# Golay bits of four tiles in one product, one row mean, paired chances, a reordered setup and later leads

## The chip, the cores and the metric

The kernel runs on one core of a Trainium2 chip. The metric is the device time of one execution, in microseconds (us), median of several runs. Engines: PE multiplies matrices, DVE and ACT work element by element, POOL issues the gathers and scatters by index, SP issues the plain DMAs. Every engine works through its own instructions in order and waits on semaphores of the others.

## The reference

x is 16 x 1024 x 512, that is 16384 tokens. D is one scalar, made from the first 1024 elements.

```python
xn = _layernorm(x, axis=-1)
x1 = jnp.fft.ifft(jnp.fft.fft(xn, axis=-1) * filt(D), axis=-1).real
bits = (sigmoid(x1 @ W_el + b_el) > 0.5)                  # 24 a token
syn = (bits @ _H.T > 0.5)                                 # 12 a token
corrected = where(0 < syn.sum(-1) <= 3, bits flipped at the set places, bits)
s = x1 + corrected @ W_le + b_le
probs = softmax(xn @ router_w.T)                          # 8 experts, two chosen
w = topk_vals / (topk_vals.sum(-1, keepdims=True) + 1e-06)
g = silu(sum over the two of (xn @ expert_w[e] + probs[e]) * w[e])
out = x + s * g
```

## The kernel before

The 16384 tokens are 128 tiles of 128 tokens; a block is TPT = 4 tiles, a group GT = 8 tiles, a routing round 16 tiles.

**Setup** finds D, and from it the filter's matrices cs, cd and cm, whose first columns also give the 24 code logits and the 8 router logits. `constants` and `more_constants` fill small tables; `setup` issues the rest in an order written by hand, with the first tiles' `total`, `spread`, `fold` and `transpose` among it.

**Pass 1** (`pass_1`, L1050 on) takes the tiles in turn. Per tile: `total` adds the halves of x and the row's sum on DVE (L431); `spread` squares on ACT for the variance (L451); `level` makes two scalings of four tiles' sums, k.low = -4/E times the sum (L444) and the mean, column 10 of the record (L445); `scale` gives the reciprocal deviation; `fold` makes sums and differences, sd on DVE (L490, L493) and mm on POOL (L495); `transpose` turns these four blocks on PE (L502) and ACT copies them to pmt (L504); `filt` multiplies on PE (L518, L519, L521) and ACT scales the result into yb (L524); each block is stored to yd, which also starts a load of a later block and, for the first eight, of one expert's weights. How far totals and spreads run ahead is set by AHEAD_S = 11 and by a ramp at the start (2g+13 and 2g+12).

The Golay code, `code(s)`, is worked once a group: bits (L560), `turn_bits` for four tiles at a time (one matmul of 24 columns a tile, L569, and one ACT copy, L572), `syndrome` (one matmul a tile, L579), `correct` (L583 to L593). Its steps go out one a tile. `route(n)` goes out up to four steps a tile: the two largest logits, the softmax's chances and weights, 28 pair indicators (L709, one product for each distance between experts), sums over four tiles (L723), each token's rank in its pair's list by PE (L731 to L755), place (L762), row numbers (L767), and then 16 scatters to `lists` (L771). `put_records` stores the records.

**Pass 2** (the loop on L1383) first works `whole` tiles, 128 tokens of one pair of experts: two products of four f32 matmuls, PE L1228, scaled on ACT (L1275), added on DVE (L1278), silu on ACT (L1279). Leftover tokens go by expert: 61 `item` tiles with one product each, stored to ed; later `rest` tiles gather these parts. The order is 28 whole, 61 items, 5 whole, then 27 rest among 68 whole. Each step issues for later tiles: entries of the lists (AHEAD_K = 9 tiles ahead), x rows (6), parts (4), yd rows (5), `normalize` (L1189, 4), `turn` (four transposes and ACT's xt copy, L1196 and L1198, 2 ahead). `turn_code` turns the corrected bits (L1249, copy ct L1253), `mend` multiplies by W_le, `spread_out` joins the parts of x1 on DVE, `combine` and `put` finish and scatter the rows. `routes` and `aside` hold list work that goes out one or more steps a tile at the start of pass 2.

The changed kernel has functions of the same names; the diff below says what is in them.

Of the kernel before, what the change touches and what calls it, by code (L numbers as in the profile page):

```python
# [17 lines left out]
P = 128  # L18
PSUM = bass.MemoryType.PSUM
DRAM = bass.MemoryType.DRAM  # L20
NPAIR = 28
# [6 lines left out]
def pairs_of(ne=8):  # L28

    return [(a, a + d) for d in range(1, ne) for a in range(ne - d)]  # L30
# [3 lines left out]
def kernel(  # L34
# [114 lines left out]
    ht_b = p1c.tile([L, 12], BF16, name="ht_b")  # L149
# [15 lines left out]
    ht = sp.tile([L, 12], F32, name="ht")  # L165
# [23 lines left out]
    def constants():  # L189
# [26 lines left out]
        kf = kf[:, 0:KC]  # L216
# [13 lines left out]
        v.memset(eps, EPS)  # L230

    def more_constants():
# [11 lines left out]
        for r in recs:  # L244
            g.memset(r, 0.0)
            g.memset(bits_of(r)[:, :, L : L + 1], 1.0)
        for py in pys:
            v.memset(py[:, 1, X + H : WY], 0.0)

    def setup():  # L250
# [19 lines left out]
        nc.tensor.matmul(pm[:, NS - 1 :], st.own, sums[:, NS - 1 :], start=True, stop=True)  # L270
        above = sp.tile([P, NS, HW], F32, name="above")
# [7 lines left out]
        nc.tensor.matmul(pn, st.all, cnt, start=True, stop=True)  # L279
        ly = sp.tile([P, NS], F32, name="ly")  # L280
        v.tensor_scalar(ly, pn, 1.0, None, ALU.max)
        nc.scalar.activation(ly, ly, AF.Ln)
# [19 lines left out]
        v.tensor_sub(wt[:, 2:4, :], lat[:, 0:2, :], lat[:, 2:4, :])  # L302
        gain = sp.tile([P, KC], F32, name="gain")
# [10 lines left out]
        for i in range(2):  # L314
            for c in range(2):
                nc.tensor.matmul(
                    pys[1][:, i, 0:H], bas[:, 2 + c, i * P : (i + 1) * P], gbas[:, 2 + c, :],
                    start=(c == 0), stop=(c == 1),
                )
        v.tensor_add(wt[:, 0, :], wp[:, 0, :], wp[:, 1, :])  # L320
        v.tensor_sub(wt[:, 1, :], wp[:, 0, :], wp[:, 1, :])
        for g in range(2):
            total(g)
            spread(g)
        nc.scalar.copy(cs[:, X:], pys[0][:, 0, 0:Q])
        nc.scalar.copy(cd[:, X:], pys[0][:, 1, 0:Q])
        for g in range(2, 4):
            total(g)
            spread(g)
        level()  # L330
        nc.scalar.copy(cm[:, :, X:], pys[1][:, :, 0:H])
# [3 lines left out]
        fold(0)  # L335
# [12 lines left out]
        for op in scale(0, slice(0, TPT)):  # L348
            op()
# [3 lines left out]
        for g in range(4, GT):  # L353
            total(g)
            spread(g)
        level()
# [65 lines left out]
    def total(g: int):  # L422

        k, j = groups[g // GT], g % GT
        if j == 0:
            k.sum = small.tile([P, GT], F32, name="sum")
            k.sq2 = small.tile([P, GT], F32, name="sq2")
            k.low = small.tile([P, GT], F32, name="low")
# [12 lines left out]
    def level():  # L441
        while means:
            k, js = means.pop()
            nc.scalar.activation(k.low[:, js], k.sum[:, js], AF.Copy, scale=-4.0 / E)  # L444
            nc.scalar.activation(k.rec[:, js, 10], k.sum[:, js], AF.Copy, scale=1.0 / E)  # L445
# [38 lines left out]
    def fold(g: int):  # L484
# [6 lines left out]
            sd[:, 0:Q], p[:, 0:Q], k.low[:, j : j + 1], p[:, Q:H], ALU.add, ALU.add  # L491
# [61 lines left out]
    def code(s: int):  # L553
# [3 lines left out]
        def bits():  # L557

            k.bits = bits_of(k.rec)[:, :, 0:L]
# [4 lines left out]
        def turn_bits(h):  # L564
            if h == 0:
                k.bt = small.tile([L, GT, P], BF16, name="bt", bufs=2)
            pg = ps_g.tile([P, 512], F32, name="pg")[0:L].rearrange("l (j t) -> l j t", t=P)
            for j in range(TPT):
                nc.tensor.matmul(  # L569
                    pg[:, j, :], k.bits[:, h + j, :], ident_b, start=True, stop=True  # L570
                )
            nc.scalar.copy(k.bt[:, h : h + TPT, :], pg)  # L572

        def syndrome():
            k.pg = ps_g.tile([P, 512], F32, name="pg")[:, 0 : GT * 12].rearrange(
                "p (j n) -> p j n", n=12
            )
            for j in range(GT):
                nc.tensor.matmul(k.pg[:, j, :], k.bt[:, j, :], ht_b, start=True, stop=True)  # L579

        def correct():
# [12 lines left out]
                k.bits[:, :, 0:12], k.bits[:, :, 0:12], fix, ALU.not_equal  # L594
# [20 lines left out]
    def route(n: int):  # L615
# [30 lines left out]
        def total():  # L646
            st.sm = new("sm", [P, S])
# [886 lines left out]
```

## Time and profile before

| | |
|---|---|
| four runs | 1461.28, 1461.63, 1444.55, 1458.19 us; median 1459.74 |
| profiled execution | 1460.7 us, of which 1458.8 are its span; mean granted clock 0.967 |
| PE, DVE, POOL, ACT busy | 1344.1, 924.3, 876.7, 604.1 us |
| read from HBM, written | 144.79 MB, 87.75 MB |

A window row gives a stretch and its length, then for each engine its busy time and the number of instructions, PE's granted clock (1.00 is full), the share of DMA and what it moved in GB/s. The whole span in six stretches: setup, the DMA-bound tiles, the other tiles of pass 1, the start of pass 2 with 28 whole tiles, the items, the rest.

```profile
0.00:40.00 40.00, 24.68 (x121) 20.78 (x122) 28.62 (x135) 29.04 (x78) 13.46 (x44) 0.91 0.63 217
40.00:120.86 80.86, 77.89 (x491) 62.31 (x490) 71.23 (x262) 73.85 (x179) 40.53 (x48) 0.98 1.01 342
120.86:312.00 191.14, 184.97 (x1179) 146.87 (x1178) 174.67 (x642) 172.20 (x410) 146.57 (x162) 0.98 0.70 219
312.00:606.00 294.00, 250.63 (x781) 124.22 (x780) 175.84 (x460) 77.23 (x139) 154.34 (x146) 0.93 0.33 98
606.00:866.00 260.00, 242.07 (x740) 119.22 (x739) 41.94 (x84) 65.81 (x124) 117.82 (x117) 0.97 0.43 131
866.00:1458.80 592.80, 563.83 (x1641) 271.42 (x1639) 432.01 (x1058) 185.93 (x369) 403.99 (x365) 0.98 0.52 156
```

Engine columns: PE, PE's weight loads, DVE, ACT, POOL.

### The profile page before, as it was taken

How to read it: one execution, taken by the hardware profiler on the slowest of the kernel's cores; microseconds unless marked ns; L12 is line 12 of the kernel's file. 1: busy time of each engine (PE TensorE's matmuls, PEld its weight loads, DVE VectorE, ACT ScalarE, POOL GpSimd, SP SyncE). 2: the span in 40 equal slices, each digit the busy share in tenths (PEclk: the TensorE clock that was granted, in tenths of full speed). 3: DMA queues.
4: the chain of work that ended last, by engine and by line, in shares of the span. 5: the costliest groups of instructions: out<-in, count | busy, mean ns of one | idle time of the engine just before them, and what ended most of it. 6: DMA issues, size and time to landing. Idle time of an engine off the chain costs nothing.

```text
span 1458.8 us, 18162 instructions
## 1 busy us (share of the span) xinstructions
PE 1344.1 (92%) x4944; PEld 744.8 (51%) x4944; DVE 924.3 (63%) x2635; ACT 604.1 (41%) x1298; POOL 876.7 (60%) x879
## 2 busy tenths in 40 slices
PE   5999999896597999959999999999899899999996
PEld 4877777773243444424444444444444444444443
DVE  6898999774354688701111126778677677777784
ACT  7989999773121222212222232333233233333332
POOL 3366877676356455565554216777777677777741
PEclk9999999998799999989999999999999999999998
DMA  5998787544223332344445425555555555555531
GB/s 209 371 299 293 247 244 242 166 158 142 60 68 94 111 101 87 102 116 138 138 133 160 139 89 146 174 165 174 162 164 171 151 171 172 172 165 171 178 122 43
DMA packets 119215, 233.75 MB, mean 160 GB/s; under 512 B 37355, under 2 KB 71019, under 8 KB 115022
## 3 DMA queue, kind: packets, MB, share of 16 engines
q0 software_dynamic: 47264, 135.54, 31.8%
q1 hardware_dynamic: 71386, 96.88, 19.8%
q8 instruction: 43, 0.70, 0.2%
q14 instruction: 54, 0.44, 0.1%
q10 hardware_dynamic: 468, 0.19, 0.1%
HBM read 144.79 MB, written 87.75 MB: 159 GB/s over the span
## 4 chain that ended last, share of the span: by engine, by line
PE 55%; issue 15%; DVE 10%; POOL 9%; another core or an unknown queue 5%; ACT 3%; DMA 2%; POOLq 0%; DVEq 0%; ACTq 0%; SPq 0%
PE pe L1228 38%; PE py L521 5%; PE pt L1196 4%; POOL out L1312 3%; PE pt L502 2%; POOL yg L1135 2%; POOL xg L1135 2%; PE py L518 1%; PE py L519 1%; POOL part L1135 1%; DVE pp L431 1%; DVE sd L490 1%; DMA yd<-yb 1%; POOL entry L1135 1%
## 5 line engine op out<-in xcount | busy, mean ns | idle before, releaser
L1228 PE MATMUL pe<-w_sb,xt 128*128 x2104 | 951.7, 600 | 3.6 <-issue 2.3
L1228 PEld LDWEIGHTS pe<-w_sb,xt 128*128 128x128 f32 x2104 | 399.3, 193 | 428.4 <-issue 421.3
L1279 ACT ACTIVATE acc<-acc,yg 128x512 f32<-128x512 f32 x128 | 92.4, 722 | 420.8 <-DVE acc L1278 324.8
L1278 DVE SCALAR_TENSOR_TENSOR acc<-pe,yg,acc 128x512 f32<-128x512 f32 x101 | 75.7, 749 | 242.8 <-PE pe L1228 144.5
L1198 ACT COPY xt<-pt 128x512 f32<-128x512 f32 x162 | 93.8, 579 | 210.5 <-PE pt L1196 164.9
L1135 POOL DMA_INDIRECT yg<-yd,toks x101 | 112.4, 1113 | 113.9 <-ACT acc L1279 50.8
L1312 POOL DMA_INDIRECT out<-xg,toks x101 | 110.7, 1096 | 82.0 <-DVE xg L1307 55.5
L1189 DVE TENSOR_SCALAR xn<-xg,entry 128x512 f32<-128x512 f32 x61 | 34.2, 561 | 196.5 <-PE pt L1196 159.5
L771 POOL DMA_INDIRECT lists<-rec,dst x128 | 133.6, 1043 | 34.1 <-issue 22.2
L495 POOL TENSOR_TENSOR mm<-xt 128x256 f32<-128x256 f32 x128 | 100.2, 783 | 84.8 <-PE pt L502 64.3
L1196 PEld LDWEIGHTS pt<-ident,xn 128*128 128x128 f32 x648 | 81.8, 144 | 132.9 <-issue 93.2
L521 PE MATMUL py<-cm,pmt 128*128 128x288 f32 x512 | 147.7, 412 | 0.0
L1196 PE MATMUL pt<-ident,xn 128*128 128x128 f32 x648 | 100.8, 279 | 44.7 <-ACT xt L1198 27.0
L1275 ACT ACTIVATE acc<-pe,yg 128x512 f32<-128x512 f32 x101 | 68.9, 682 | 160.4 <-PE pe L1228 82.6
L1135 POOL DMA_INDIRECT xg<-in_x,toks x101 | 108.9, 1079 | 40.7 <-issue 28.9
L524 ACT ACTIVATE yb<-py,rec 128x640 f32<-128x640 f32 x128 | 101.6, 794 | 30.1 <-PE py L521 21.5
L1135 POOL DMA_INDIRECT xg<-in_x,entry x88 | 90.6, 1030 | 29.5 <-issue 26.4
L1135 POOL DMA_INDIRECT entry<-lists,adr_i x61 | 62.9, 1032 | 64.3 <-DVE xn L1189 50.7
L1135 POOL DMA_INDIRECT part<-ed,adr_r x54 | 62.0, 1148 | 65.0 <-DMA ed<-res 48.8
L521 PEld LDWEIGHTS py<-cm,pmt 128*128 128x128 f32 x512 | 91.9, 193 | 13.9
L1307 DVE TENSOR_TENSOR xg<-mix,xg 128x512 f32<-128x512 f32 x128 | 88.5, 692 | 4.9 <-issue 0.4
L451 ACT ACTIVATE no<-xt,sum 128x512 bf16<-128x512 f32 x128 | 91.0, 711 | 1.2 <-DVE pp L431 1.2
(270 smaller groups left out, 1763.1 us busy)
## 6 DMA issues: line engine op xcount, KB each, us to landing
xt<-in_x SPq DMA_DIRECT2D x32, 1024.0 KB
yd<-yb SPq DMA_DIRECT2D x32, 576.0 KB
yd<-yb SPq DMA_DIRECT2D x32, 512.0 KB
ed<-res SPq DMA_DIRECT2D x61, 256.0 KB
w_sb<-in_expert_w SPq DMA_DIRECT2D x8, 1024.0 KB
yd<-rec SPq DMA_DIRECT2D x36, 64.0 KB
lists<-rec,dst POOLq DMA_INDIRECT x128
xg<-in_x,toks POOLq DMA_INDIRECT x101
```

Of the source, the lines that this page charges most:

```text
L451: nc.scalar.activation(no, xts[g // TPT][:, g % TPT, :], AF.Square, bias=k.sum[:, j : j + 1], scale=-float(E), accum_out=k.sq2[:, j : j + 1],)
L495: nc.gpsimd.tensor_tensor(m, xr[:, 0:H], xr[:, H:E], ALU.subtract)
L521: nc.tensor.matmul(py[:, 1, 0 : X + H], pmt[:, 2 + c, :], cm[:, c, :], start=(c == 0), stop=(c == 1))
L524: nc.scalar.activation(y_room(g), py[:, :, 0:WY], AF.Copy, scale=k.rec[:, j, 11:12])
L771: dma = nc.gpsimd.indirect_dma_start(out=lists, out_offset=bass.IndirectOffsetOnAxis(ap=st.dst[:, j : j + 1], axis=0), in_=st.rec.bitcast( ...
L1135: nc.gpsimd.indirect_dma_start(out=dst, out_offset=None, in_=src, in_offset=bass.IndirectOffsetOnAxis(ap=idx, axis=0), bounds_check=limit - 1,
L1196: nc.tensor.transpose(pt[:, c * P : (c + 1) * P], k.xn[:, c * P : (c + 1) * P], ident)
L1198: nc.scalar.copy(k.xt.rearrange("p c t -> p (c t)"), pt)
L1228: nc.tensor.matmul(pe.unsqueeze(1), k.xt[:, c, :], w_sb[:, bass.ds(e, 1), c, :], start=(c == 0), stop=(c == KC - 1),)
L1279: nc.scalar.activation(k.acc, k.acc, AF.Silu, bias=k.rec[:, 9:10])
L1307: nc.vector.tensor_add(k.x, k.mix, k.x)
L1312: dma = nc.gpsimd.indirect_dma_start(out=of, out_offset=bass.IndirectOffsetOnAxis(ap=k.tok, axis=0), in_=k.x, in_offset=None, bounds_check ...
```

## The change

Five parts. (1) Golay: the bits of four tiles are turned by one matmul of 96 columns, the syndrome takes one matmul for four tiles with a block-diagonal matrix, bits lie in a tile of their own, and ACT copies the last 12 of them to the records. (2) One row mean: k.low goes, the record's column 10 holds -4/E times the sum, and the two readers in pass 2 multiply by -0.25. (3) Routing: pairs are numbered cyclically, so four products make the 28 indicators; the sum over four tiles is two additions; chances and weights of both experts lie side by side. (4) Setup is reordered, the records are cleared by DVE instead of POOL, the ramp is 2g+8 and 2g+7. (5) Pass 2: AHEAD_K, X, N and T are 10, 7, 5 and 3; `turn` goes by a list of due steps; items turn in PSUM tiles of ps_g once routes and aside are empty; `turn_code` has a ring of four slots; the lists begin one step later.

```diff
--- before
+++ after
@@ -27,7 +27,8 @@
-    return [(a, a + d) for d in range(1, ne) for a in range(ne - d)]
+    near = [(a, (a + d) % ne) for d in range(1, ne // 2) for a in range(ne)]
+    return [tuple(sorted(k)) for k in near] + [(a, a + ne // 2) for a in range(ne // 2)]
@@ -146,7 +147,7 @@
     bel_r = row_sb[:, 3 * NPAIR :]
-    ht_b = p1c.tile([L, 12], BF16, name="ht_b")
+    ht_b = p1c.tile([TPT * L, TPT * 12], BF16, name="ht_b")
@@ -162,7 +163,7 @@
     lat = sp.tile([P, KC, X], F32, name="lat")
-    ht = sp.tile([L, 12], F32, name="ht")
+    ht = sp.tile([TPT * L, TPT * 12], F32, name="ht")
@@ -213,7 +214,11 @@
             v.memset(st.slope[:, i : i + 1], -(n * x_ - sum(lx)) / den)
-        kf = kf[:, 0:KC]
+        v.memset(eps, EPS)
+        st.kf = kf[:, 0:KC]
+    def arguments():
+        v, kf = nc.vector, st.kf
@@ -227,7 +232,6 @@
         v.tensor_scalar(st.by0[:, 1, :], ka, -1.0, -0.5 * math.pi, ALU.mult, ALU.add)
-        v.memset(eps, EPS)
@@ -241,11 +245,10 @@
             g.memset(iota_e[:, e : e + 1], float(e))
-        for r in recs:
-            g.memset(r, 0.0)
-            g.memset(bits_of(r)[:, :, L : L + 1], 1.0)
-        for py in pys:
-            v.memset(py[:, 1, X + H : WY], 0.0)
+    def clear(r):
+        nc.vector.memset(r, 0.0)
+        nc.vector.memset(bits_of(r)[:, :, L : L + 1], 1.0)
@@ -268,6 +271,7 @@
         nc.tensor.matmul(pm[:, NS - 1 :], st.own, sums[:, NS - 1 :], start=True, stop=True)
+        arguments()
@@ -277,8 +281,11 @@
         nc.tensor.matmul(pn, st.all, cnt, start=True, stop=True)
+        clear(recs[0])
...
+        for py in pys:
+            v.memset(py[:, 1, X + H : WY], 0.0)
@@ -300,6 +307,7 @@
         v.tensor_sub(wt[:, 2:4, :], lat[:, 0:2, :], lat[:, 2:4, :])
+        total(0)
@@ -317,22 +325,21 @@
                 )
+        for g in range(1, 4):
+            total(g)
...
-        for g in range(2):
-            total(g)
-            spread(g)
+        spread(0)
+        level()
+        fold(0)
+        spread(1)
...
-        for g in range(2, 4):
-            total(g)
-            spread(g)
-        level()
-        nc.scalar.copy(cm[:, :, X:], pys[1][:, :, 0:H])
...
-        fold(0)
+        spread(2)
+        nc.scalar.copy(cm[:, :, X:], pys[1][:, :, 0:H])
@@ -345,15 +352,21 @@
                 )
-        for op in scale(0, slice(0, TPT)):
-            op()
+        spread(3)
+        fold(1)
+        begin, middle, end = scale(0, slice(0, TPT))
+        begin()
...
-        for g in range(4, GT):
-            total(g)
-            spread(g)
-        level()
+        middle()
+        transpose(1)
+        end()
+        total(4)
+        spread(4)
+        clear(recs[1])
+        total(5)
+        spread(5)
@@ -425,7 +438,6 @@
             k.sq2 = small.tile([P, GT], F32, name="sq2")
-            k.low = small.tile([P, GT], F32, name="low")
@@ -441,8 +453,7 @@
             k, js = means.pop()
-            nc.scalar.activation(k.low[:, js], k.sum[:, js], AF.Copy, scale=-4.0 / E)
-            nc.scalar.activation(k.rec[:, js, 10], k.sum[:, js], AF.Copy, scale=1.0 / E)
+            nc.scalar.activation(k.rec[:, js, 10], k.sum[:, js], AF.Copy, scale=-4.0 / E)
@@ -488,7 +499,7 @@
         nc.vector.scalar_tensor_tensor(
-            sd[:, 0:Q], p[:, 0:Q], k.low[:, j : j + 1], p[:, Q:H], ALU.add, ALU.add
+            sd[:, 0:Q], p[:, 0:Q], k.rec[:, j, 10:11], p[:, Q:H], ALU.add, ALU.add
@@ -556,27 +567,30 @@
         def bits():
-            k.bits = bits_of(k.rec)[:, :, 0:L]
+            k.bits = small.tile([P, GT, L], BF16, name="bits", bufs=2)
             nc.vector.tensor_tensor(
                 k.bits, k.ex[:, :, 0:L], negb.unsqueeze(1).to_broadcast([P, GT, L]), ALU.is_gt
             )
         def turn_bits(h):
             if h == 0:
-                k.bt = small.tile([L, GT, P], BF16, name="bt", bufs=2)
-            pg = ps_g.tile([P, 512], F32, name="pg")[0:L].rearrange("l (j t) -> l j t", t=P)
-            for j in range(TPT):
+                k.bt = small.tile([TPT * L, GT // TPT, P], BF16, name="bt", bufs=2)
+            pg = ps_g.tile([P, 512], F32, name="pg")[0 : TPT * L, 0:P]
+            nc.tensor.matmul(
+                pg, k.bits[:, h : h + TPT, :].rearrange("p j l -> p (j l)"), ident_b, start=True, stop=True
+            )
+            nc.scalar.copy(k.bt[:, h // TPT, :], pg)
+        def syndrome():
+            pg = ps_g.tile([P, 512], F32, name="pg")[:, 0 : GT * 12]
+            k.pg = pg.rearrange("p (j n) -> p j n", n=12)
+            nc.scalar.copy(bits_of(k.rec)[:, :, 12:L], k.bits[:, :, 12:L])
+            for h in range(GT // TPT):
                 nc.tensor.matmul(
-                    pg[:, j, :], k.bits[:, h + j, :], ident_b, start=True, stop=True
+                    pg[:, h * TPT * 12 : (h + 1) * TPT * 12], k.bt[:, h, :], ht_b,
+                    start=True, stop=True,
                 )
-            nc.scalar.copy(k.bt[:, h : h + TPT, :], pg)
-        def syndrome():
-            k.pg = ps_g.tile([P, 512], F32, name="pg")[:, 0 : GT * 12].rearrange(
-                "p (j n) -> p j n", n=12
-            )
-            for j in range(GT):
-                nc.tensor.matmul(k.pg[:, j, :], k.bt[:, j, :], ht_b, start=True, stop=True)
         def correct():
             syn = small.tile([P, GT, 12], F32, name="syn")
@@ -591,7 +605,7 @@
             nc.vector.tensor_tensor(
-                k.bits[:, :, 0:12], k.bits[:, :, 0:12], fix, ALU.not_equal
+                bits_of(k.rec)[:, :, 0:12], k.bits[:, :, 0:12], fix, ALU.not_equal
@@ -645,6 +659,10 @@
             st.sm = new("sm", [P, S])
+            st.den = new("den", [P, S])
+            st.ch = small.tile([P, 2, S], F32, name="ch", bufs=1)
+            st.wt = small.tile([P, 2, S], F32, name="wt2", bufs=1)
@@ -679,8 +697,10 @@
         def chosen():
-            st.sel = new("sel", SN, BF16)
-            v.tensor_add(st.sel, st.hot1, st.hot2)
+            st.sel = new("sel", [P, S, NE + NE // 2], BF16)
+            v.tensor_add(st.sel[:, :, 0:NE], st.hot1, st.hot2)
+            v.tensor_copy(st.sel[:, :, NE:], st.sel[:, :, 0 : NE // 2])
@@ -688,17 +708,14 @@
-        def den_of():
-            st.den = new("den", [P, S])
-            v.tensor_add(st.den, st.sm, st.p2)
...
-            lambda: v.reciprocal(st.sm, st.sm),
-            lambda: v.tensor_mul(st.p2, st.p2, st.sm),
-            den_of,
-            lambda: v.tensor_scalar(st.den, st.den, 1e-6, None, ALU.add),
+            lambda: v.reciprocal(st.ch[:, 0, :], st.sm),
+            lambda: v.tensor_mul(st.ch[:, 1, :], st.p2, st.ch[:, 0, :]),
+            lambda: v.scalar_tensor_tensor(
+                st.den, st.ch[:, 0, :], 1e-6, st.ch[:, 1, :], ALU.add, ALU.add
+            ),
@@ -706,23 +723,22 @@
                 st.oh = new("oh", [P, S, NPAIR], BF16)
+            n = min(NE, NPAIR - at)
...
-                st.oh[:, :, at : at + NE - d], st.sel[:, :, 0 : NE - d], st.sel[:, :, d:NE]
-            )
-        at = 0
-        for d in range(1, NE):
-            ops.append(lambda d=d, at=at: pair(d, at))
-            at += NE - d
+                st.oh[:, :, at : at + n], st.sel[:, :, 0:n], st.sel[:, :, d : d + n]
+            )
+        for d in range(1, NE // 2 + 1):
+            ops.append(lambda d=d: pair(d, (d - 1) * NE))
...
-            with nc.allow_low_precision("counts up to 4"):
-                v.tensor_reduce(
-                    st.q4, st.oh.rearrange("p (a b) k -> p a k b", b=4), AX.X, ALU.add
-                )
+            o4 = st.oh.rearrange("p (a b) k -> p a b k", b=4)
+            two = small.tile([P, 4, 2, NPAIR], BF16, name="q2", bufs=1)[:, 0:A]
+            v.tensor_add(two, o4[:, :, 0:2, :], o4[:, :, 2:4, :])
+            v.tensor_add(st.q4, two[:, :, 0, :], two[:, :, 1, :])
@@ -784,30 +800,26 @@
         def weigh():
-            st.w1 = new("w1", [P, S])
-            v.tensor_mul(st.w1, st.sm, st.den)
-            st.w2 = new("w2", [P, S])
-            v.tensor_mul(st.w2, st.p2, st.den)
+            v.tensor_mul(st.wt, st.ch, st.den.unsqueeze(1).to_broadcast([P, 2, S]))
...
-            v.tensor_mul(st.sm, st.sm, st.w1)
-            v.tensor_mul(st.p2, st.p2, st.w2)
+            v.tensor_mul(st.ch, st.ch, st.wt)
...
-            v.tensor_sub(st.den, st.w1, st.w2)
+            v.tensor_sub(st.den, st.wt[:, 0, :], st.wt[:, 1, :])
...
-            lambda: v.tensor_add(st.rec[:, :, 9], st.sm, st.p2),
+            lambda: v.tensor_add(st.rec[:, :, 9], st.ch[:, 0, :], st.ch[:, 1, :]),
...
-            lambda: v.tensor_add(st.rec[:, :, 0], st.w2, st.lo),
-            lambda: v.tensor_sub(st.rec[:, :, 1], st.w1, st.lo),
+            lambda: v.tensor_add(st.rec[:, :, 0], st.wt[:, 1, :], st.lo),
+            lambda: v.tensor_sub(st.rec[:, :, 1], st.wt[:, 0, :], st.lo),
@@ -917,7 +929,10 @@
             nc.vector.tensor_copy(toks[part], k.pt[:, 2, :])
-            nc.vector.tensor_copy(stats[part], k.pt[:, 0:2, :])
+            nc.vector.tensor_scalar(
+                stats[part][:, 0, :], k.pt[:, 0, :], -0.25, None, ALU.mult
+            )
+            nc.vector.tensor_copy(stats[part][:, 1, :], k.pt[:, 1, :])
@@ -936,7 +951,7 @@
-        aside.extend([lengths, None, full, None, rows_, None, where, upto, None, bounded])
+        aside.extend([None, lengths, None, full, None, rows_, None, where, upto, None, bounded])
@@ -1063,9 +1078,11 @@
         rest = setup_code()
-        scales += scale(0, slice(TPT, GT))
-        totals, spreads = list(range(GT, NT)), list(range(GT, NT))
+        totals, spreads = list(range(6, NT)), list(range(6, NT))
...
+            if g == 4:
+                clear(recs[2])
+                clear(recs[3])
@@ -1075,21 +1092,22 @@
                 take_ex(g // TPT - 1)
-            if 0 < g + 2 < NT:
+            if g < 0:
+                continue
+            if g + 2 < NT:
...
-            while totals and totals[0] <= g + AHEAD_S + 1 and totals[0] <= 2 * g + GT + 5:
+            while totals and totals[0] <= g + AHEAD_S + 1 and totals[0] <= 2 * g + GT:
...
-            while spreads and spreads[0] <= g + AHEAD_S and spreads[0] <= 2 * g + GT + 4:
+            while spreads and spreads[0] <= g + AHEAD_S and spreads[0] <= 2 * g + GT - 1:
...
-                if spreads.pop(0) % GT == GT - 1:
-                    scales += scale((g + AHEAD_S) // GT)
-            if 0 < g + 1 < NT:
+                s, j = divmod(spreads.pop(0), GT)
+                if j == GT - 1:
+                    scales += scale(s, slice(TPT, GT)) if s == 0 else scale(s)
+            if 1 < g + 1 < NT:
...
-            if g < 0:
-                continue
@@ -1112,7 +1130,7 @@
-    AHEAD_K, AHEAD_X, AHEAD_P, AHEAD_Y, AHEAD_N, AHEAD_T = 9, 6, 4, 5, 4, 2
+    AHEAD_K, AHEAD_X, AHEAD_P, AHEAD_Y, AHEAD_N, AHEAD_T = 10, 7, 4, 5, 5, 3
@@ -1123,6 +1141,7 @@
     room = w2.tile([P, 512], F32, name="room", bufs=1)
+    pcs = ps_c.tile([96, 4, P], F32, name="pc")
@@ -1158,7 +1177,7 @@
         k.tok = entry[:, 2:3]
-        k.mean, k.scale = (entry.bitcast(F32)[:, i : i + 1] for i in range(2))
+        k.low, k.scale = (entry.bitcast(F32)[:, i : i + 1] for i in range(2))
@@ -1186,12 +1205,19 @@
         k.xn = w1.tile([P, E], F32, name="xn2")
+        if k.kind == "item":
+            k.mean = w2.tile([P, 1], F32, name="mean1", bufs=2)
+            nc.vector.tensor_scalar(k.mean, k.low, -0.25, None, ALU.mult)
...
-        pt = ps_x.tile([P, KC * P], F32, name="pt2")
+        if k.kind == "item" and not (routes or aside):
+            pt = ps_g.tile([P, KC * P], F32, name="pg")
+        else:
+            pt = ps_x.tile([P, KC * P], F32, name="pt2")
@@ -1245,7 +1271,7 @@
             return
-        pc = ps_c.tile([96, P], F32, name="pc")
+        pc = pcs[:, k.at % 4, :]
@@ -1338,11 +1364,12 @@
         tiles.append(Tile(kind, seen.get(kind, 0)))
+        tiles[-1].at = len(tiles)
...
-    routes += route(len(rounds) - 1) + [lambda: whole_ops(1)] + [None] * 5
+    routes += route(len(rounds) - 1) + [lambda: whole_ops(1)] + [None] * 6
@@ -1364,6 +1391,7 @@
     due = {
+        "turn": [max(k - AHEAD_T, min(k - 2, 3)) for k in range(NTILE)],
@@ -1372,7 +1400,7 @@
     def those(n, name, op):
-        k = range(max(0, n - 2), min(NTILE, n + 5)) if n >= 0 else ()
+        k = range(max(0, n - 2), min(NTILE, n + 5))
@@ -1397,7 +1425,7 @@
             def beside():
-                each(n + AHEAD_T, turn)
+                those(n, "turn", turn)
@@ -1443,6 +1471,10 @@
     golay_t[12:] = np.eye(12)
+    golay_4 = np.zeros((96, 48), np.float32)
+    for j in range(4):
+        golay_4[24 * j : 24 * j + 24, 12 * j : 12 * j + 12] = golay_t
@@ -1515,7 +1547,7 @@
         "basis": basis,
-        "golay_t": golay_t,
+        "golay_t": golay_4,
```

## The prediction

> **What bounds the kernel now.** I read the windows first, cut at stages and at rounds of 16 tiles.
>
> ```profile
> 120.86:156.89 36.03, 36.01 (x235) 28.81 (x234) 32.40 (x121) 34.78 (x84) 28.89 (x33) 1.00 0.81 252
> 156.89:194.75 37.86, 36.32 (x235) 28.87 (x234) 37.03 (x130) 35.21 (x84) 29.08 (x33) 1.00 0.75 237
> 194.75:231.66 36.91, 36.12 (x235) 28.81 (x234) 35.93 (x128) 35.01 (x85) 29.32 (x33) 1.00 0.79 244
> 231.66:269.33 37.67, 37.66 (x246) 29.50 (x245) 36.59 (x147) 34.88 (x85) 29.97 (x33) 1.00 0.76 239
> ```
> Columns: stretch and its length, then busy time (instructions) of PE, PE's weight loads, DVE, ACT, POOL, then granted clock, DMA share, GB/s. The reader is to see three engines full together: PE 36.0 to 37.7 us of a mean round of 37.1, DVE 35.5 on the mean, ACT 35.0. Work must leave all three.
>
> ```profile
> 16.00:40.00 24.00, 18.47 (x103) 15.97 (x104) 18.65 (x77) 21.38 (x62) 7.14 (x8) 0.86 0.48 168
> 40.00:80.00 40.00, 39.98 (x256) 31.97 (x255) 35.37 (x128) 38.97 (x95) 14.21 (x18) 1.00 1.01 354
> 345.00:460.00 115.00, 76.05 (x227) 35.45 (x226) 50.85 (x157) 25.29 (x46) 62.16 (x60) 0.86 0.26 72
> 660.00:866.00 206.00, 206.00 (x642) 101.79 (x641) 31.61 (x62) 57.23 (x108) 81.34 (x81) 1.00 0.42 131
> 866.00:1458.00 592.00, 563.83 (x1641) 271.42 (x1639) 432.01 (x1058) 185.93 (x369) 403.99 (x365) 0.98 0.52 157
> ```
> Before 40 us ACT is the full engine; from 40 to 120 us DMA (share 1.01); items are PE throughout (206.00 of 206). PE is idle 39 us in 345 to 460 and 28 us in the last 592.
>
> The waits of PE, window 16 to 121, then 345 to 460, then 606 to 660, then 866 to the end, say who ended these idle times:
>
> ```profile
> PE pt L502 <- DVE sd L490: 5.5, 2, 5.1
> PE pc L1249 <- ACT ct L1253: 23.7, 3, 22.3
> PE pt L1196 <- issue: 9.2, 1, 9.2
> PE pt L1196 <- ACT xt L1198: 8.8, 1, 8.8
> PE pt L1196 <- ACT xt L1198: 10.3, 7, 4.0
> ```
>
> **Start.** Of the first row, 5.1 us are one wait: fold(0) stood on DVE behind spreads and totals, and PE idled from 18.8 to 23.9 us. The change puts fold(0), fold(1) and transpose(1) ahead, moves the eight argument operations out of DVE's opening stretch, and delays totals and spreads: 8 instead of 12 spreads (0.71 busy plus 0.1 to 0.19 read-out, 0.81 each) stand before tile 0's filter, but 14 instead of 15 before tile 3's. Tile 0 could thus gain 5 us, yet ACT is full, so the ramp returns most of it: at tile 3, where the first store leaves, one spread (0.8), two small level scalings (0.2) and an ACT start some 2 us earlier remain, 3.0. Bounds: 1 (the clears of DVE, 2 to 4 operations near 0.5, and the new ACT order eat it) and 4.5. The DMA-bound stretch doesn't swallow it: DMA is idle half of 16 to 40 us and its full stretch begins with the first store at 34.6 us, which moves along. Speed-ups *inside* that stretch, tiles 4 to 36, are swallowed (at tile 36 the chain of waits has 12.2 us of DMA), so I count 5.5 rounds, tiles 40 to 128, not 8.
>
> On the cold start: 24 to 28 us shows a granted clock of 0.54 and tile 0's transposes and products take 3.99 us on the chain against 1.95 later. [...]
>
> **A round.** The rows that carry it, PE, ACT, DVE groups by form in 121 to 269 us:
>
> ```profile
> L569 PE MATMUL pg<-ident_b,rec 128*24 128x128 bf16 x64 | 6.3, 221 | 0.2 <-DVE pl L762 0.2
> L579 PE MATMUL pg<-ht_b,bt 24*128 24x12 bf16 x64 | 2.8, 165 | 0.0
> L572 ACT CAST bt<-pg 24x512 bf16<-24x512 f32 x16 | 8.9, 558 | 0.0
> L444 ACT ACTIVATE low<-sum 128x4 f32<-128x4 f32 x16 | 3.2, 198 | 0.0
> L723 DVE TENSOR_REDUCE q<-oh 128x112 bf16<-128x448 bf16 x4 | 3.7, 930 | 0.1
> L801 DVE TENSOR_TENSOR den<-w,w 128x16 f32<-128x16 f32 x4 | 0.7, 165 | 0.0
> L808 DVE TENSOR_TENSOR lo<-lo,den 128x16 f32<-128x16 f32 x4 | 2.7, 665 | 0.1
> ```
> - PE. A tile with the turning of four tiles' bits takes 2.42 us against 1.95 plain: 0.47 for four matmuls. One remains, somewhat wider in weights: 0.15 to 0.22, taken 0.2. Four a round: 1.1 saved. Eight syndrome matmuls add 0.37; two, with 48 columns out, 0.15 to 0.2: 0.4 saved in a round. Sum 1.5.
> - ACT. One of two level scalings goes: start to start 0.10 (row 198 ns overlapped), four a round, 0.4. The bits' copy falls from 512 to 128 columns: slot 0.46 to about 0.16 (a 96x128 cast of pass 2 lasts 0.26), four a round, 1.2. Added: two copies of 12 bits, 0.13 each. Sum 1.3.
> - DVE. Pair products 7 to 4, one copy added: 0.8 to about 0.65. One reduce (0.93) becomes two bf16 adds of 224 and 112 elements; the nearest row is a 112-element bf16 product, 0.25: 0.25 to 0.4 and 0.25, so 0.3 saved. The fused sum 0.1 to 0.17; weigh and biases 0.16 each become wider: 0.2 together. Sum 0.9; bits and correction keep their form.
>   The price that may return: of equal shape, L801 takes 165 ns and L808 665: an operation that falls under POOL's 0.78 us tensor operation is 0.5 longer. If both adds fall there, DVE saves nothing on quads and loses 0.7; so DVE's round lies between -0.1 and 1.2.
> - POOL and DMA: the same operations in a round.
>
> PE's new floor is 37.1 less 1.5; ACT's less 1.3; DVE (0.96 of the time) less about 1. I take 1.3, with 0.3 (DVE holds) and 1.5: 5.5 x 1.3 = 7.2, bounds 1.7 and 8.3.
>
> [...]
>
> **What doesn't act.** The ring of four slots for turn_code in pass 2 is one tile in PSUM, and the built kernel's second turn_code of a pair still waits on ACT's copy of the first: 0. Item tiles get one small DVE operation (0.16 to 0.25) more, 61 of them: DVE is busy 31.6 of 206 us there: 0, and 10 to 15 us if it stood on the path. The list step "kept" gets one such operation more, twice, off the path: 0.
>
> **Hand-over.** Near 291 us about 6.5 us are lost to a gather from the lists. Scatters now start a tile earlier (97 instead of 96 done when pass 1 ends), put_records an iteration earlier, "lengths" one later: 0 to 2, taken 1.
>
> **Later leads.** Turning three tiles ahead and normalizing five ahead gives no more buffers (xn and xt four each, 14 gathered x tiles, unchanged) and nothing in the items, where PE is full. On PE the transposes of n+3 instead of n+2 stand beside product n; queued behind them are that tile's remaining products, and ACT's copy goes ahead of later evictions. On POOL eight x gathers instead of seven (1.08 each) precede the first yd gather: 1.1 later there, under the first two products. Gain only where PE idles on xt: 8.8 (606 to 660) and 10.3 us (last stage) by the rows above; items turn into two other PSUM buffers there. A fifth of their 19.1 is 3.8; less the 1.1 on POOL, 2.7. Bounds -3 (three gathers at a start) and 8.
>
> **Sum.** Profiled execution: span 1458.8 and 1.9 around it, 1460.7. Less 3.0, 7.2, 1.0, 2.7 = 13.9: 1446.8. The median of the four runs, 1459.74, is 1.0 below the profiled one: 1445.8, called 1446.
>
> **Rivals.**
> 1. *Only the first pass acts* and DVE holds the rounds: 1459.7 less 3, 1.7 to 5 and 0 gives 1452 to 1455. For: DVE 37.03 of 37.86 in one round. Against: PE and ACT both shed work and DVE too.
> 2. *The number of holds shifts.* Four times in pass 2 PE's product ends some 14 us late; the last two show as
>
> ```profile
> 624.26 0.59 ACT L1287 COPY res<-pe 128x512 f32<-128x512 f32 x1
> 638.68 0.59 ACT L1198 COPY xt<-pt 128x512 f32<-128x512 f32 x1 [13.82 <-issue]
> 652.88 0.59 ACT L1198 COPY xt<-pt 128x512 f32<-128x512 f32 x1 [13.12 <-remote]
> ```
>    (the timeline of ACT). All fall while POOL issues gathers back to back, 1.31 us apart; their cause isn't established. One of four runs was 1444.55, 14 to 17 below the rest: just one such hold less. One fewer: 1432; one more: 1460. Leads that reorder POOL's gathers can do either; the matched length of the runs speaks for it.
> 3. *Slower: PE waits for a tile one further away.* In the last stage PE stands 7 times, 10.3 us, on ACT's xt. If POOL (404 of 592 us busy) lags by more than a tile's 7.57 us, the transposes of n+3 come before the loaded product of n and hold it. Were such waits four times as many, +31: 1477; it decides from about 20 more waits of 1.5 us. Against: the gather moves ahead by the same tile as the turn.
>
> **How the numbers follow.** A measurement of this kernel tells about 1% from no change: faster means under 1445.1, slower over 1474.3. Forecast with all terms (1440 to 1452): 0.50, about half of it under 1445.1 (0.26). Rival 1: 0.10, same. One hold fewer: 0.20, faster. One more: 0.08, same. Rival 3: 0.12, slower. Hence faster 0.46, same 0.42, slower 0.12. The range 1430 to 1463 takes the forecast, rival 1, one hold more, and most of one hold fewer; the unknown costs (gains of 0 to 23 together) give 1437 to 1460 and lie within.
>
> **What would show it.** PE's 5.1 us on sd gone, tile 3's filtered output near 31 instead of 34 us; rounds after 120 us of 35.5 to 36, PE near 34.7; bt's cast near 0.26 and L723's place two short adds, neither over 0.5; the stall at tile 36 no longer than 13 us. Holds of 13 us or more: four. Wrong if rounds stay at 37 with DVE full, if pass 2 from first to last product differs by over 10 us, or if another count of holds appears.

## The result and the profile after

The changed kernel took 1460.04 us (median of 52 runs, 1450.34 to 1475.32), the kernel before 1460.02 (78 runs, 1442.22 to 1471.31). The ratio is 1.002, 95% interval 1.0007 to 1.0034: no change by the 1% of the prediction, where 14 us of gain were forecast. Ratios here and below count only runs within 1.5% of their kernel's fastest, so they can differ from the ratio of the medians. The profiled execution took 1471.86 us (span 1470.1), 12 above its median.

The windows of the changed kernel, at the same tiles as the four rounds shown of before (stretch, then busy time of PE, its weight loads, DVE, ACT, POOL, clock, DMA share, GB/s):

```profile
117.03:152.20 35.17, 34.39 (x211) 28.31 (x210) 32.99 (x117) 33.36 (x84) 29.03 (x33) 1.00 0.85 256
152.20:190.27 38.07, 35.20 (x211) 28.09 (x210) 37.11 (x125) 34.02 (x84) 29.64 (x33) 1.00 0.78 236
190.27:228.42 38.15, 35.27 (x211) 28.14 (x210) 37.18 (x125) 34.03 (x84) 29.51 (x33) 1.00 0.76 235
228.42:267.21 38.79, 36.74 (x222) 28.94 (x221) 37.68 (x137) 33.80 (x84) 29.76 (x33) 1.00 0.75 232
```

PE and ACT did get lighter, by 1.1 and 1.2 us a round (sums 146.1 to 141.6 and 139.9 to 135.2). DVE got heavier: 142.0 to 145.0 over the four, with three to ten fewer instructions a round, and it now fills 97.1 to 97.5% of each of the last three rounds. They are longer, not shorter: 38.1, 38.2 and 38.8 against 37.9, 36.9 and 37.7.

Where DVE's time went is in its groups by form, first of before and then of after, 121 to 269 and 117 to 267 us:

```profile
L493 DVE TENSOR_TENSOR sd<-pp 128x128 f32<-128x128 f32 x64 | 22.3, 349 | 0.0
L549 DVE TENSOR_REDUCE ex<-yb 128x128 f32<-128x384 f32 x16 | 9.4, 589 | 2.3 <-ACT yb L524 2.3
L480 DVE SCALAR_TENSOR_TENSOR rec<-ln_v,ln 128x8 f32<-128x8 f32 x8 | 1.5, 182 | 0.3
```
```profile
L504 DVE TENSOR_TENSOR sd<-pp 128x128 f32<-128x128 f32 x63 | 28.6, 454 | 0.0
L560 DVE TENSOR_REDUCE ex<-yb 128x128 f32<-128x384 f32 x15 | 8.8, 585 | 1.3 <-ACT yb L535 1.3
L491 DVE SCALAR_TENSOR_TENSOR rec<-ln_v,ln 128x8 f32<-128x8 f32 x8 | 4.1, 507 | 0.3
L740 DVE TENSOR_TENSOR q<-oh 128x224 bf16<-128x224 bf16 x4 | 1.1, 275 | 0.1
L741 DVE TENSOR_TENSOR q<-q 128x112 bf16<-128x112 bf16 x4 | 0.9, 218 | 0.1
```

The two additions that replaced the reduction (L740, L741) cost what was forecast. But the second operation of `fold`, which the change doesn't touch, takes 454 ns on the mean instead of 349: 28.6 us instead of 22.3, more than the 3.6 us that DVE was to save in four rounds (0.9 each). The small operation that ends `scale` (L480, now L491) rises by another 2.6 us. The mean hides two values. DVE's timeline in a later profile of the changed kernel, and below it POOL's:

```profile
200.27 0.81 DVE L504 TENSOR_TENSOR sd<-pp 128x128 f32<-128x128 f32 x1
...
203.14 0.28 DVE L504 TENSOR_TENSOR sd<-pp 128x128 f32<-128x128 f32 x1
```
```profile
200.13 0.79 POOL L506 TENSOR_TENSOR mm<-xt 128x256 f32<-128x256 f32 x1
```

It lasts 0.28 us alone and 0.81 when it starts while POOL subtracts (200.13 to 200.92). In tiles 40 to 104 the long form occurs 20 times after the change and 7 times before. All 20 overlap POOL's subtraction: in the first profile 16 of them start 0.01 to 0.16 us behind its start and last 0.80 to 0.91 us, and four start 0.58 to 0.59 ahead of it, while POOL issues a scatter, and last 0.81 to 0.82. Of the 43 short ones 37 don't overlap it, and six do with their last 0.07 to 0.11 us; all last 0.27 to 0.29. The reduction L560 (one input in SBUF) overlaps it in 5 of 15 cases and lasts 592 ns there and 582 otherwise. The number of inputs alone doesn't tell them apart: the copy L653 has one too, and lasts 0.16 us alone and 0.59 to 0.76 in the three of four cases that overlap. A meeting thus costs `fold`'s operation 0.53 us, near the 0.5 that the prediction read from L801 and L808, but the price falls on this operation and not on the two additions.

Tile by tile, from ACT's scaling into yb, the gain over before is 5.6 us at tile 0, 3.0 at tile 3, 3.8 at tile 40, 4.7 at 56, 2.1 at 104 and 3.4 at 127. In this profile it is 6.1 after the 28 whole tiles and 10.7 after the items (three holds where before had four), and then the last stage loses 22. PE's largest wait there, 860 us to the end, before and after:

```profile
PE pt L1196 <- ACT xt L1198: 10.3, 7, 4.0
```
```profile
PE pt L1222 <- ACT xt L1224: 27.2, 9, 3.9
```

These waits come one in each seven tiles or so, some 3 us each.

One thing is needed to read what follows: the experiments ran in other sessions, in most of which the kernel before took 1372 us, in one 1446. The section on hardware shows where the difference lies: in pass 2. Each ratio below is therefore with runs of the kernel before in its own session.

### The profile page after: what moved, and what is told of

It reads as the page before. It is cut to its first block, busy times and chain, and to the rows that moved or that the text cites. A ratio compares the mean times of both kernels' runs of the same rounds, so it can differ in the third digit from the quotient of the medians.

```text
span 1470.1 us, 17755 instructions
## 1 busy us (share of the span) xinstructions
PE 1333.0 (91%) x4752; PEld 738.0 (50%) x4752; DVE 936.7 (64%) x2674; ACT 593.6 (40%) x1282; POOL 871.3 (59%) x871
## 4 chain that ended last, share of the span: by engine, by line
PE 56%; DVE 15%; issue 10%; ACT 6%; another core or an unknown queue 5%; DMA 4%; POOL 3%; SPq 0%; POOLq 0%; ACTq 0%; DVEq 0%
PE pe L1254 47%; PE pt L1222 2%; DMA yd<-yb 2%; DVE pp L443 2%; PE pg L1222 2%; ACT no L462 2%; DVE sd L504 2%; DVE sd L501 2%; POOL out L1338 1%; ACT yb L535 1%; PE pg L1287 1%; PE py L532 1%; ACT pmt L515 1%; DVE acc L1304 1%
## 5 line engine op out<-in xcount | busy, mean ns | idle before, releaser
L1338 POOL DMA_INDIRECT out<-xg,toks x101 | 109.4, 1083 | 82.8 <-DVE xg L1333 56.5
L787 POOL DMA_INDIRECT lists<-rec,dst x128 | 135.6, 1059 | 37.7 <-issue 21.6
L1211 DVE TENSOR_SCALAR xn<-xg,mean,entry 128x512 f32<-128x512 f32 x61 | 33.8, 555 | 185.4 <-PE pg L1222 135.7
L1222 PE MATMUL pt<-ident,xn 128*128 128x128 f32 x424 | 65.8, 279 | 45.9 <-ACT xt L1224 39.7
L1222 PEld LDWEIGHTS pt<-ident,xn 128*128 128x128 f32 x424 | 52.7, 143 | 104.6 <-issue 51.7
L1224 ACT COPY xt<-pg 128x512 f32<-128x512 f32 x56 | 32.8, 586 | 174.6 <-PE pg L1222 127.9
L532 PEld LDWEIGHTS py<-cm,pmt 128*128 128x128 f32 x512 | 91.9, 193 | 13.9
```

Source lines behind the costliest of these rows:

```text
L532: nc.tensor.matmul(py[:, 1, 0 : X + H], pmt[:, 2 + c, :], cm[:, c, :], start=(c == 0), stop=(c == 1))
L787: dma = nc.gpsimd.indirect_dma_start(out=lists, out_offset=bass.IndirectOffsetOnAxis(ap=st.dst[:, j : j + 1], axis=0), in_=st.rec.bitcast( ...
L1222: nc.tensor.transpose(pt[:, c * P : (c + 1) * P], k.xn[:, c * P : (c + 1) * P], ident)
L1338: dma = nc.gpsimd.indirect_dma_start(out=of, out_offset=bass.IndirectOffsetOnAxis(ap=k.tok, axis=0), in_=k.x, in_offset=None, bounds_check ...
```

## The experiments

**Pass 1 or the leads.** Four kernels. `p1_only` puts pass 2 back, `leads_only` adds only the fifth part to the kernel before, and two put back one pair of leads in the changed kernel:

```diff
-    AHEAD_K, AHEAD_X, AHEAD_P, AHEAD_Y, AHEAD_N, AHEAD_T = 10, 7, 4, 5, 5, 3
+    AHEAD_K, AHEAD_X, AHEAD_P, AHEAD_Y, AHEAD_N, AHEAD_T = 9, 6, 4, 5, 4, 2      # p1_only, and the rest of part 5
+    AHEAD_K, AHEAD_X, AHEAD_P, AHEAD_Y, AHEAD_N, AHEAD_T = 10, 7, 4, 5, 4, 2     # nt_back
+    AHEAD_K, AHEAD_X, AHEAD_P, AHEAD_Y, AHEAD_N, AHEAD_T = 9, 6, 4, 5, 5, 3      # kx_back
```

> The first four parts of the change with pass 2 as before (leads 9, 6, 4, 2; turn by its lead; no second set of turning buffers; lists not delayed). Theory A, the leads cost what pass 1 gains: the first pass ends 2 to 4 us earlier, the last stage has no periodic holes of 3 us (five or fewer over 1.2 us, before had five), and the time is 1451 to 1456. Theory B, pass 1's gain dies at the start of pass 2 whatever the leads are: 1458 to 1462, as the changed kernel.

> The kernel before with the fifth part of the change alone (leads 10, 7, 5, 3, turning buffers of items, lists one step later). Theory A: one hole of about 3 us in each period of seven tiles of the last stage, 10 or 11 in all, 1463 to 1470. Theory B: the last stage keeps its five holes and the time is that of before, 1458 to 1462.

> The changed kernel with normalize and turn at their old leads, 4 and 2, entries and x rows at the new 10 and 7. If turning three tiles ahead makes the periodic holes (the transposes of a tile meet a rest tile's short step at another place), they go and the time is 1450 to 1456. If the order of POOL's gathers makes them, they stay, 10 or 11 of 3 us, and the time is 1458 to 1464.

> The changed kernel with entries and x rows at their old leads, 9 and 6, normalize and turn at the new 5 and 3. The mirror of the run before: if POOL's order makes the holes, they go and the time is 1450 to 1456; if turning ahead makes them, they stay and the time is 1458 to 1466.

Measured: p1_only 1.0028 (1.0015 to 1.0041), leads_only 0.9978 (0.9969 to 0.9988), nt_back 0.9978 (0.9969 to 0.9987), kx_back 0.9983 (0.9973 to 0.9993). Theory A falls on both sides: the leads gain 0.22%, the first four parts lose 0.28%. Theory B isn't supported either: p1_only's pass 1 brought no gain that could be lost later, its tile 127 coming at 328.2 us (before: 329.4 and, in a second profile, 326.3). None of the four has a hole of PE over 1.2 us in the last stage, and neither has the kernel before in these sessions. So the leads alone don't make the holes of the first profile; whether they do in a session with holds, nt_back and kx_back can't tell.

**Without POOL's subtraction.** In both kernels a tile of zeros stands for mm:

```diff
-        m = front.tile([P, H], F32, name="mm")
-        nc.gpsimd.tensor_tensor(m, xr[:, 0:H], xr[:, H:E], ALU.subtract)
-        pms[g] = sd, m
+        pms[g] = sd, still
```

> The changed kernel without POOL's subtraction of the halves (mm); a tile of zeros is turned in its place, so the odd frequencies are left out of the filter. Theory A, the gain of a round was lost because DVE's operations with two SBUF inputs wait while POOL's subtraction runs: the second operation of fold falls from 454 ns on the mean to about 285 in every tile, and a round of 16 tiles behind tile 56 falls from 38.3 to 34 to 35.5 us. Theory B, DVE or another engine is full without that: the mean falls by less than 50 ns and the round stays over 37.

> The kernel before with the same left out. Theory A: rounds of 35 to 36.5 us behind tile 56, so that the changed kernel's rounds are 1.0 to 1.5 us shorter without the contention, as its removed work says. Theory B: rounds of both differ by less than 0.5.

Measured, one run each: 1365.07 and 1369.11 us, before 1373.73. `fold`'s second operation takes 285 and 284 ns on the mean, and DVE's busy time in a round falls to about 27 and 28 us. So the lengthening is POOL's. The rounds didn't follow: 36.9, 41.4, 43.3 and 36.2 us in after_nomm, 37.3 to 37.9 in before_nomm, with a DMA share of 0.87 to 0.98; ACT waited 14.5 us for stores of yd in after_nomm. Both theories miss on the rounds: as a price of the contention in time, this experiment is inconclusive.

**Setup and leads, or the rounds.** Profiles of both kernels in one session, and the change split the other way: `start_leads` has parts 4 and 5, `rounds_only` parts 1 to 3.

> The kernel before once more, for a profile beside these runs. Theory H, the 85 us between the first profile and the runs of this study are holds of PE in pass 2: pass 1 ends within 5 us of 329 us, no product of pass 2 is held for over 5 us, the plain whole tile keeps 7.57 us and the item 3.87, 1369 to 1376. Its rival: pass 1 or the pitch of the tiles is shorter too.

> The changed kernel beside it. If the parts add up as p1_only (+0.28%) and leads_only (-0.22%) measured, 1370 to 1375 and a ratio of 0.999 to 1.002; if turning ahead costs something beside the new first pass (nt_back was 0.9978), 1373 to 1378.

> The kernel before with the new setup and the new leads, but with Golay, row mean and routing as before. Theory C, the new rounds cost DVE what they save PE and ACT: pass 1 ends 2 to 4 us before that of leads_only (324.4), and the time is 1364 to 1368. Theory D, the new setup spoils the order behind it: pass 1 ends at 326 or later, 1369 to 1374.

> The kernel before with the new Golay, row mean and routing alone, old setup and leads. Theory C: the rounds behind tile 56 last 37.5 to 38.5 us, fold's second operation means over 420 ns, and the time is 1374 to 1379. Theory D: rounds of 36.5 us or less and 1364 to 1370.

Measured: before_b 0.9997 (0.9988 to 1.0006), after_b 0.9986 (0.9977 to 0.9995), start_leads 0.9963 (0.995 to 0.9975), rounds_only 1.0042 (1.0029 to 1.0055). Pass 1 ended (tile 127) at 326.3, 327.0, 323.0 and 330.7 us. Theory H stands (the windows are in the section on hardware). after_b came just under its expected 1370 to 1375 us, with 1369.88. Theory C stands: the parts made to relieve the rounds lose 5.8 us, though start_leads ended pass 1 only 1.4 us before leads_only (2 to 4 expected). In rounds_only the operation means 461 ns and the rounds behind tile 56 last 38.1, 38.1 and 39.0 us. The first profiles' rounds repeat to 0.05 us here, so rounds can be compared between sessions. Tiles 104 to 112, where the lists are gathered, don't: the kernel before took 24.6 us for them in its first profile and 21.8 in before_b.

**Which of the three.** One part at a time on start_leads, and the changed kernel with three buffers for sd and mm:

```diff
-        sd = front.tile([P, H], F32, name="sd")
+        sd = front.tile([P, H], F32, name="sd", bufs=3)
...
-        m = front.tile([P, H], F32, name="mm")
+        m = front.tile([P, H], F32, name="mm", bufs=3)
```

> start_leads with the new Golay code. Theory G: with the turning tile 0.4 us shorter on PE, the transposes free POOL's buffer earlier and POOL's subtraction falls on fold's second operation; that operation means over 400 ns in tiles 40 to 104 (start_leads 344), rounds behind tile 56 are 37 to 38.5, 1369 to 1374. Rival R, routing is to blame: mean near 344, rounds 0.8 to 1.5 shorter than those of start_leads (36.9, 37.0, 37.8), 1358 to 1363.

> start_leads with one row mean. Both theories: one small ACT operation less each four tiles, ACT isn't the last to arrive, rounds within 0.3 of start_leads, 1364 to 1369. If reading the record's column instead of a tile of its own adds a wait, rounds grow by 0.5 or more and 1369 to 1374.

> start_leads with the new routing. Theory G: DVE about 1 us a round less, rounds 0.3 to 1 shorter than those of start_leads, 1360 to 1365. Rival R: the two additions and the wider products, with two inputs in SBUF where a reduction had one, fall under POOL's subtraction; the tile with the ranks (3.3 us in start_leads, 3.9 in the changed kernel) lasts 3.6 or more, rounds over 37.5, 1368 to 1374.

> The changed kernel with three buffers instead of two for sums (sd) and differences (mm). If the overlap follows from the release of these buffers by the transposes, the phase of POOL's subtraction changes: fold's second operation leaves its 454 ns by more than 50 and the rounds change by more than 0.5, either way. If DVE, late by itself, sets when it meets the subtraction, 430 to 480 ns, rounds of 37.8 to 38.8, 1368 to 1372.

| | ratio (interval) | round from tile 40, 56, 72, 88 | second operation of fold, long ones | pass 1 ends |
|---|---|---|---|---|
| start_leads | 0.9963 (0.995 to 0.9975) | 36.03, 36.91, 37.00, 37.82 | 344 ns, 7 | 322.96 |
| start_golay | 0.9916 (0.9897 to 0.9936) | 34.72, 37.49, 37.48, 38.28 | 386 ns, 10 | 320.86 |
| start_mean | 0.9947 (0.9926 to 0.9967) | 35.93, 37.87, 36.85, 37.82 | 349 ns, 7 | 324.11 |
| start_route | 0.9986 (0.9974 to 0.9998) | 36.10, 37.76, 37.76, 38.51 | 457 ns, 19 | 327.54 |
| mm3 | 1.0035 (1.0023 to 1.0047) | 38.04, 39.14, 39.17, 39.82 | 524 ns, 23 | 332.99 |

Theory G, which blamed Golay, falls: with it alone the time is the best of all. Yet part of it came: the three rounds behind tile 56 are 0.5 us longer each, as long as G said, with ten long operations for seven, and only the round from tile 40 is shorter. What start_golay gains in pass 1 lies in tiles 104 to 112 (19.7 us against 24.5). Rival R stands as to the part: routing alone takes start_leads from 0.9963 to 0.9986, and the long operations from 7 to 19. Of R's own signs the tile with the ranks came (3.7 us). In start_mean the round from tile 56 missed its expected 0.3 us: it is 1.0 longer, 37.87, which is what the kernel before has with the same routing (37.86). mm3 shows that when the buffers come free matters, but more of them makes the overlap worse.

**What in the routing.** `route_reduce` puts the reduction back; `route_pad` adds an empty step to the list. The shorter list had moved the ranks from the last tile of the round to the one before it.

```diff
-        ops += [quads, None, rank]
+        ops += [None, quads, None, rank]      # route_pad, and after_pad on the changed kernel
```

> start_route with the reduction over four tiles back in place of the two additions. Theory Q, the additions have two inputs in SBUF and wait for POOL: fold's second operation falls from 457 to under 380 ns and rounds behind tile 56 to 37.2 or less, 1364 to 1367. Theory P, the place in the list: nothing but 0.3 us a round longer on DVE, mean over 430, rounds of 37.7 to 38.2, 1369 to 1373.

> start_route with one empty step ahead of the sum over four tiles, so that the ranks fall in the same tile of the round as in start_leads. Theory P: rounds of 36.0 to 37.2 behind tile 56, fold's second operation under 390 ns, 1362 to 1367. Theory Q: rounds stay at 37.5 to 38.5 and the mean over 430, 1368 to 1372.

> The whole change without the new routing: start_golay with one row mean. If the parts add up (start_golay -0.84%, one row mean -0.16%), 1356 to 1361 and a ratio of 0.989 to 0.992. If one row mean meets the contention as routing did, 1361 to 1366.

The times are inconclusive, since this was the session with 1446 us: 0.9993 (0.9947 to 1.0039), 1.0002 (0.9945 to 1.0059) and 1.0013 (0.9977 to 1.0049); golay_mean missed its 0.989 to 0.992. Nor do they follow pass 1: its last tile came at 331.7, 325.1 and 319.4 us in the three profiles, and the medians are 1439.4, 1440.0 and 1441.6 (before 1446.1). So 12 us in pass 1 don't show in the totals beside the 1446 us. Pass 1 itself isn't inconclusive. The windows of start_route's first two rounds, and of route_pad's:

```profile
117.64:153.74 36.10, 36.03 (x235) 28.84 (x234) 31.77 (x118) 34.74 (x86) 28.91 (x33) 1.00 0.82 249
153.74:191.50 37.76, 36.57 (x235) 28.86 (x234) 36.80 (x124) 35.27 (x86) 29.78 (x33) 1.00 0.77 238
```
```profile
119.99:156.08 36.09, 35.97 (x235) 28.73 (x234) 32.38 (x118) 34.78 (x85) 28.62 (x33) 1.00 0.84 252
156.08:192.17 36.09, 35.97 (x235) 28.73 (x234) 34.16 (x124) 34.79 (x85) 29.08 (x33) 1.00 0.84 248
```

The same instructions on every engine (x124 on DVE), and DVE busy 34.2 instead of 36.8 us: PE is full again (35.97 of 36.09). The four rounds last 36.09, 36.09, 36.29 and 37.82, the operation means 359 ns with 8 long ones. Theory P stands. Theory Q, and with it R's reason, falls: with the reduction back it means 466 ns and the middle rounds last 38.13, 0.4 more than with the additions. In golay_mean the rounds are those of start_golay (34.76, 37.44, 37.47, 38.23): beside the new Golay code one row mean adds nothing that shows in them.

**The whole change with the empty step.**

> The changed kernel with one empty step ahead of the sum over four tiles, nothing else. If the place of the ranks is what took the gain, fold's second operation falls from 454 to under 400 ns, the round from tile 40 is 34.7 to 35.2 and the next two are 35 to 36.5 instead of 38.1, pass 1 ends 4 to 7 us before the changed kernel's 326 to 327, and on a chip where before takes 1372 the time is 1358 to 1365. If with the shorter Golay code the overlap stays wherever the ranks are, the rounds stay at 37.5 to 38.2 and the time within 3 us of the changed kernel's.

Measured: 1361.02 us against 1371.82, ratio 0.9936 (0.9919 to 0.9953). Pass 1 ends at 318.1, 8.9 us before after_b (4 to 7 expected). Windows of after_b, then after_pad, two rounds each:

```profile
152.90:190.98 38.08, 35.20 (x211) 28.09 (x210) 37.12 (x125) 34.01 (x83) 29.63 (x33) 1.00 0.83 236
190.98:229.12 38.14, 35.27 (x211) 28.16 (x210) 37.17 (x125) 34.04 (x84) 29.50 (x33) 1.00 0.78 235
```
```profile
153.75:190.67 36.92, 34.55 (x211) 28.23 (x210) 36.06 (x124) 33.82 (x82) 29.48 (x33) 1.00 0.83 243
190.67:227.61 36.94, 34.55 (x211) 28.22 (x210) 36.08 (x124) 33.82 (x82) 29.52 (x33) 1.00 0.82 243
```

Each middle round is 1.2 us shorter, and tiles 104 to 112 take 19.3 instead of 25.0 us. The waits of PE from 260 to 345 us, after_b and after_pad, name what changed there:

```profile
PE pt L513 <- POOL mm L506: 6.0, 2, 4.6
```
```profile
PE pt L513 <- POOL mm L506: 1.0, 1, 1.0
```

The overlap fell less than expected (432 ns, 15 long ones, not under 400), and the middle rounds missed the upper bound of 36.5 by 0.4: DVE is still the fullest engine. The time is in the expected range. after_pad and start_golay (0.9916) both beat both kernels; which of the two is faster their sessions don't settle.

## Why the prediction was wrong

- **Start, 3.0 us: right.** Tile 3 came 3.0 us earlier (33.82 to 30.81), 3.3 in the second pair, tile 0 5.6; the DMA-bound stretch moved along (3.8 at tile 40) and swallowed what was gained inside it (5.1 at tile 32). The granted clock, for which the forecast has no term, was 0.54 at 24 to 28 us and 1.00 at 28 to 32 before, 0.78 and 0.80 after; PE's longest wait from 16 to 40 us was 5.1 us before and 2.1 after.
- **A round, 1.3 us: wrong, and this is the step that failed.** PE's and ACT's terms were near (1.5 and 1.3 forecast, 1.1 and 1.2 measured). DVE's was set at "between -0.1 and 1.2" saved; it lost 0.75. The prediction had the price of one meeting right (0.5 us), but counted it only for the operations that the change adds, 0.7 us if both additions met POOL. Those didn't. It was above all `fold`'s own operation, 128 times in pass 1, that met POOL's subtraction thirteen times more in four rounds, about 0.53 us each, once the list of steps was four shorter and the ranks fell a tile earlier. The prediction listed that shift under the hand-over alone, as scatters and records one tile earlier. Over tiles 40 to 104 the rounds gave back 1.7 us instead of gaining 5.2 (1.3 x 4).
- **Hand-over, 1.0: unsettled in sign.** In the first pair tiles 104 to 127 gain 1.3; in the second they lose 2.6. Most of the swing is the kernel before's own: it took 60.1 us there in its first profile and 56.5 in before_b.
- **Later leads, 2.7: right in size where there are no holds.** leads_only measures 2.4 (medians 1372.16 and 1369.79). Between the ends of pass 1 and of the 28 whole tiles the second pair gains 4.7 us; items and last stage keep their pitch to 0.5, so the gain is in the start, not in the waits on xt of which the prediction took a fifth. Right by luck, then; and in the profile of the session that the forecast was made for, the waits on xt of the last stage grew, from 10.3 to 27.2 us.
- **The rivals.** The first, DVE holds the rounds, was the mechanism; it was given a tenth, because DVE's work was counted and not the time it stands, and even it still had a gain of 1.7 to 5 us where 1.7 were lost. The second, holds, may explain the scatter of single runs, though no run shows it; it doesn't explain why the first profile lies 12 us above its median, since that has a hold less. The third, PE waiting for a tile one further away, did show in that profile: 27.2 us on ACT's xt in the last stage, 16.9 more than before, in nine waits where it spoke of 28 shorter ones. In after_b PE has no such wait over 1 us. The three kernels with these leads in the session at 1446 have it once at most (4.3 us in golay_mean). How much of it the median of the 52 runs holds isn't known.
- **The sum.** With 13.9 forecast, the second pair shows start -3.7 (at tile 40), rounds +1.7, tiles 104 to the end of pass 1 +2.6, then -5.2: 4.6 in spans, 0.14% in the ratio. In the session of the result the medians show nothing even of this. The sum takes for granted that what pass 1 gains reaches the end. Where there are no holds it does; in the other session with holds 12 us in pass 1 left the totals where they were, and the result's profile lost 22 us in the last stage. So the rounds are the term that failed, but that the total stood still in that session has a further cause that these runs leave open.

What is shown: one empty step, which puts the ranks and all that stands behind them in the list back by a tile, takes 4.0 us off the four rounds of after_b and 3.8 off those of start_route. With it the changed kernel's rounds are 2.3 us shorter than those of the kernel before, of 5.2 forecast; the rest stays lost, with 15 long operations left. What stays open: why a tile's shift changes how often POOL and DVE meet. The rounds repeat to 0.05 us, which speaks for a fixed pattern of the two orders, but no experiment changed the meeting alone. The 5.7 us of tiles 104 to 112 rest on one profile.

## What to carry to other kernels

Where two engines contend, count an operation's neighbours as well as its length: a step that gets shorter moves everything behind it, and the price may fall on an operation that nobody touched (here `fold`'s second, 349 to 454 ns on the mean). When a list of steps is shortened inside a loop that hands out so many a tile, check what tile the heavy ones fall in, and try empty steps before giving the saving up. An engine near full (here DVE, 96% before and 97% after) can set the round whatever is taken from its neighbours.

## What the runs showed of the hardware

The same kernel took 1372 us in most sessions and 1446 to 1460 in others. Pass 1 is nearly the same in both (tile 104 at 269.3 and 269.8 us, tile 127 at 329.4 and 326.3), and so are the pitch of whole tiles and items (7.57 and 3.87). The windows of the start of pass 2 and of the last stage, first profile of before and then before_b:

```profile
330.00:600.00 270.00, 229.80 (x670) 109.80 (x671) 163.28 (x426) 65.66 (x122) 138.88 (x129) 0.92 0.31 92
...
860.00:1350.00 490.00, 476.19 (x1392) 230.06 (x1391) 359.23 (x885) 155.78 (x311) 353.75 (x320) 0.99 0.56 165
```
```profile
330.00:600.00 270.00, 262.66 (x784) 126.25 (x785) 177.66 (x452) 74.91 (x139) 167.48 (x157) 0.99 0.38 114
...
860.00:1350.00 490.00, 490.00 (x1450) 238.12 (x1450) 387.11 (x952) 164.60 (x329) 365.60 (x328) 1.00 0.56 170
```

In the first, PE is idle 40 us of the start's 270 and 14 of the later 490; in the second 7 and none. The 14 us holds of the prediction's second rival are gone in before_b, while POOL issues the same gathers and their packets last as long (mean 145.5 and 145.1 ns on its queue, 330 to 600 us). By the record's numbering the chip was the same, 10, for the session with 1446 us and for the last one, with 1372. What holds PE in some sessions wasn't found.
